# Statistics of the 2x2 sums moved in part beside the output projection, their loads into buffers of their own, and the order of the convolution's first loads

## The chip, the core and the metric

The kernel runs on one NeuronCore of a Trainium2 chip. The core has five engines that each work through an instruction stream of their own: TensorE (PE, matmul), VectorE (DVE), ScalarE (ACT), GpSimd (POOL) and SyncE (SP, which here only issues transfers). The metric is the device time of one execution in microseconds. The kernel before takes 3109.46 us, the median of three runs (3108.26 to 3110.49).

## What is computed

Two layers follow each other on one image `x` of 384 channels and 192 x 192 pixels in float32. Cut to what matters:

```python
# layer 0: attention over channels, on the group-normalised image, added to x
qkv = einsum(gn(x), w_qkv)                  # 1152 channels, then 2x2 max pooling to 96 x 96
q, k, v = split(depthwise_3x3(qkv))
out = sum_i topk_softmax(q @ k.T) @ v * a_i # 8 heads of 48 channels
out = repeat_2x2(gelu(out))                 # back to 192 x 192
x = x + einsum(out, w_proj) + b_proj
# layer 1: large-kernel depthwise convolution, on the group-normalised x, added to x
y = gn(x)
x = x + sum_i bn_i(depthwise(y, w_i))       # a 13 x 13 kernel and six smaller ones, folded into one
```

The second group norm needs mean and variance of the new `x`. The added term is constant over each 2x2 square, so the kernel gets the variance from three things: the variance of the old `x`, the statistics of the 2x2 sums of the normalised old `x`, and the statistics of these sums (scaled) plus the projection's output. No pass over the full-size new image is needed for it.

## The kernel before

Channels lie in three thirds of 128 partitions. The order of each stage is written out by hand, inside `manual_schedule` blocks; where such a block ends and another begins, the order on each engine is set when the kernel is built, and the waits with it. [...]Tiles come from pools of on-chip memory; the space of a closed pool is given to later pools, and the first user of the new tiles then waits for the last users of the old.

1. **Statistics** of `x` for the first norm.
2. **q, k, v** (`project`, L350): 1x1 projection, pooling, depthwise taps, Gram matrices, 48 blocks of rows twice over. Beside it GpSimd writes the 2x2 sums to DRAM (`sums`, L339).
3. **Attention stage** (L739 to L766): 24 blocks of four rows (`NBB` = 24, `NBK` = 384 pixels). For a block, PE multiplies four times (`av`, L747, two PSUM buffers for each), ACT applies Gelu (L756, L758) and writes three thirds back to `v`; the rest goes through a `gx` tile (three buffers), from which ACT copies one part (L761) and VectorE two (L763). VectorE also takes the statistics of the sums: `load_sums` (L716) reads all three thirds of a block into an `sm` tile (three buffers, loaded two blocks ahead), and three `bn_stats` (L766) follow the copies. After the blocks, L771 to L779 reduce them to `mvs`, `quarter` and `pre`. The weights `wp` of the next stage are loaded on SP between the second and the third `sm`.
4. **Projection** (L1058 to L1117): for each third `i` and block `b`, PE makes `pj` (three matmuls, L1067, three PSUM buffers), ACT writes `pj` plus bias to a `pjs` tile and to DRAM (`pd`), and VectorE makes `cell` = scaled sums plus `pj` (L1082) and its statistics (L1083). The sums come a second time, third by third, into five `smj` buffers of the pool `by` (`load_sum`, L1054), four loads ahead. `derive(i)` turns a third's statistics into the norm's scale and shift, in steps spread over the next third's blocks by `advance()`: its first step is an aggregate and an addition on VectorE (L834, L835), two blocks later comes a small matmul on PE (L106). `derive(2)` begins when the blocks are over and goes on beside the convolution. In the last third also the first two pieces of the convolution are made ready: rows are loaded (`load_rows`), the projection is added (`residual`), ACT normalizes them (`normalize1`, L963), VectorE transposes them (`arrange`, L978).
5. **Convolution** (L1136 to L1157): 48 pieces `k` of eight channels `c`. For a channel PE multiplies the folded taps `wt` with the transposed rows `xp` (L996) into one of four PSUM buffers, and ACT evicts it with a bias into `co` (L1004). For piece `k+1` or `k+2`, SP loads rows (`raw` from `x`, `up` from `pd`, 1.3 and 0.6 MB) and taps (1.6 MB), GpSimd adds (L955), ACT normalizes, VectorE transposes and adds the shift's term to the taps (`patch`, L945); GpSimd sends the output of the piece before. Taps 1 are the first load on SP after the projection, rows 2 follow.

## Time and profile before

| | |
|---|---|
| median of three runs | 3109.46 us |
| the profiled execution, its own time | 3107.91 us |
| its span (first to last instruction) | 3106.1 us |
| granted clock, mean | 0.997 |
| attention stage, first matmul | 1943.97 us after the span's start |
| projection, first matmul | 2010.70 us |
| convolution, first matmul | 2170.61 us |
| mean of a statistic L766 | 0.54 us |
| landing of a load: `sm`, `smj` (medians) | 5.0 us, 2.5 us |
| DMA busy share in the convolution, 2300 to 3075 us | 0.98 |

A row of a timeline is: start in us, length in us, engine, line, operation, output and input tiles, count of merged instructions, and in brackets the idle time of the engine just before it with what ended that. The profile counts each of these float32 matmuls as two records, so a block of the projection is six. In the answer by windows a row is: window, its length, busy time of the engine (records), the clock that was granted to TensorE (1.00 is full), the busy share of the DMA engines and GB/s.

### The profile page before, as it was taken

The page shows a single profiled execution, that of the slowest core. Times are in us where ns is not written, and L with a number is a line of the kernel's source. Part 1 is how long each engine was busy: PE and PEld are TensorE (multiplying, and loading weights), DVE is VectorE, ACT ScalarE, POOL GpSimd, SP SyncE. Part 2 cuts the span into 40 slices and gives each one's busy share as a digit, 9 for nine tenths or more (in the row PEclk, how much of TensorE's full clock was granted, in tenths as well). Part 3 has the DMA queues.
Part 4 walks back from the last instruction along what each step waited for, and adds up shares of the span by engine and source line. Part 5 has one row for each costly group of instructions (what it writes and reads, how often), then busy time and mean ns, then how long its engine had stood idle before and what let it go on. Part 6 is the DMA issues. An engine that isn't in the chain of part 4 may idle for free.

```text
span 3106.1 us, 31918 instructions
## 1 busy us (share of the span) xinstructions
PE 2917.1 (94%) x10794; PEld 1939.0 (62%) x10794; DVE 2523.7 (81%) x3453; ACT 1243.4 (40%) x2339; POOL 914.1 (29%) x1103
## 2 busy tenths in 40 slices
PE   0099999999999999999999999999999999999998
PEld 0056666666666666666555555555777777777776
DVE  8968787878787878888999999868778777777775
ACT  0034444444444444444444444623333333333332
POOL 3033232423232332312222222500333333333331
PEclk9999999999999999999999999999999999999999
DMA  9933433434242424333333332776999999999994
GB/s 387 379 112 99 132 116 112 136 95 153 80 151 78 154 88 142 106 117 112 105 100 100 129 102 69 215 218 198 258 264 248 244 244 247 247 249 242 243 219 116
DMA packets 279363, 528.67 MB, mean 170 GB/s; under 512 B 26850, under 2 KB 193824, under 8 KB 279200
## 3 DMA queue, kind: packets, MB, share of 16 engines
q1 hardware_dynamic: 207936, 331.72, 39.6%
q0 software_dynamic: 45040, 151.32, 16.1%
q10 hardware_dynamic: 26224, 43.59, 3.8%
q8 instruction: 86, 1.41, 0.2%
q14 instruction: 77, 0.63, 0.1%
HBM read 365.18 MB, written 161.37 MB: 170 GB/s over the span
## 4 chain that ended last, share of the span: by engine, by line
PE 85%; DVE 10%; DMA 3%; issue 1%; POOL 0%; ACT 0%; SPq 0%; DVEq 0%; ACTq 0%; POOLq 0%
PE qkv L350 49%; PE conv L996 28%; PE pj L1067 3%; DVE stats L236 3%; DVE v L397 3%; PE gram L438 2%; PE tr L426 2%; DVE mx L361 1%; DMA xs<-in_x 1%; DMA raw<-in_x 1%; PE av L747 1%; DMA xt<-in_x 1%; DVE stats_s L766 0%; DMA smj<-sums 0%; DVE cell L1082 0%
## 5 line engine op out<-in xcount | busy, mean ns | idle before, releaser
L350 PE MATMUL qkv<-xt,wqk 128*128 128x384 f32 x3456 | 1132.5, 487 | 1.3 <-ACT xt L327 1.3
L350 PEld LDWEIGHTS qkv<-xt,wqk 128*128 128x128 f32 x3456 | 650.3, 190 | 435.7 <-ACT xt L327 2.1
L996 PE MATMUL conv<-xp,wt 128*128 128x288 f32 (+1 forms) x3840 | 917.7, 402 | 2.5 <-ACT co L1004 2.5
L996 PEld LDWEIGHTS conv<-xp,wt 128*128 128x128 f32 x3840 | 729.0, 190 | 188.8 <-ACT co L1004 2.9
L397 DVE SCALAR_TENSOR_TENSOR acc<-pooled,wd,acc 128x384 f32<-128x384 f32 (+2 forms) x1152 | 732.2, 636 | 30.6
L361 DVE TENSOR_REDUCE mx<-qkv 128x192 f32<-128x768 f32 x432 | 412.6, 955 | 241.6 <-PE qkv L350 230.0
L978 DVE STREAM_TRANSPOSE xp<-xn 128x4608 f32<-128x4608 f32 (+1 forms) x107 | 441.9, 4130 | 185.5 <-PE conv L996 165.8
L368 ACT ACTIVATE pooled<-mx,bq 128x192 f32<-128x192 f32 x432 | 196.8, 456 | 962.0 <-DVE mx L361 961.7
L350 PE MATMUL qkv<-xt,wv 128*128 128x384 f32 x1728 | 563.8, 487 | 1.7 <-ACT xt L327 1.1
L350 PEld LDWEIGHTS qkv<-xt,wv 128*128 128x128 f32 x1728 | 325.6, 190 | 234.4 <-ACT xt L327 7.5
L1004 ACT ACTIVATE co<-conv,cb 128x288 f32<-128x288 f32 x384 | 191.3, 498 | 590.6 <-PE conv L996 590.6
L335 POOL TENSOR_TENSOR sum<-xt 128x192 f32<-128x192 f32 x144 | 96.9, 673 | 1110.4 <-ACT xt L327 1098.1
L397 DVE SCALAR_TENSOR_TENSOR v<-pooled,wd,v 128x384 f32<-128x384 f32 (+2 forms) x576 | 376.6, 654 | 15.2
L327 ACT ACTIVATE xt<-xt,gn 128x768 f32<-128x768 f32 x288 | 285.1, 1014 | 2.9 <-DVE gn L244 2.9
L1021 POOL DMA_DIRECT2D out<-o x191 | 105.8, 584 | 568.3 <-DVE o L1012 518.1
L955 POOL TENSOR_TENSOR raw<-raw,up 128x2496 f32<-128x2496 f32 x46 | 230.9, 5019 | 25.7 <-DMA raw<-in_x 18.3
L1012 DVE STREAM_TRANSPOSE o<-co 128x2304 f32<-128x2304 f32 (+1 forms) x50 | 209.7, 4197 | 19.8 <-ACT co L1004 19.8
L1067 PE MATMUL pj<-v,wp 128*128 128x384 f32 x432 | 146.8, 499 | 7.8 <-DVE cell L1082 5.9
L106 PE MATMUL g_ps<-mv,gm 128*32 128x1 f32 x18 | 1.8, 185 | 154.3 <-DVE mv L240 153.6
L1067 PEld LDWEIGHTS pj<-v,wp 128*128 128x128 f32 x432 | 82.8, 194 | 64.9 <-DVE cell L1082 6.7
L236 DVE BATCH_NORM_STATS2 stats<-xs 128x6 f32<-128x512 f32 x198 | 118.2, 674 | 2.7 <-DMA xs<-in_x 2.6
L336 POOL TENSOR_TENSOR sum<-sum,xt 128x192 f32<-128x192 f32 x144 | 113.3, 787 | 11.3
(170 smaller groups left out, 1718.5 us busy)
## 6 DMA issues: line engine op xcount, KB each, us to landing
xt<-in_x SPq DMA_DIRECT2D x96, 1152.0 KB, 7.4
wt<-zd SPq DMA_DIRECT2D x47, 1536.0 KB, 13.6
raw<-in_x SPq DMA_DIRECT2D x182, 312.0 KB, 13.5
out<-o POOLq DMA_DIRECT2D x188, 288.0 KB, 7.1
zd<-v POOLq DMA_DIRECT2D x96, 416.0 KB, 4.6
up<-pd SPq DMA_DIRECT2D x184, 156.0 KB, 12.4
xs<-in_x ACTq DMA_DIRECT2D x37, 768.0 KB, 13.3
xs<-in_x SPq DMA_DIRECT2D x29, 768.0 KB, 15.0
```

Source lines behind the costliest of these rows:

```text
L236: nc.vector.bn_stats(stats[:, j, NS0 + b * (FB // 512) + q, :], xt[:, q * 512 : (q + 1) * 512])
L327: nc.scalar.activation(xt[:, j], xt[:, j], AF.Identity, bias=gn0[:, j, 1:2], scale=gn0[:, j, 0:1])
L350: nc.tensor.matmul(ps[:, r, : 2 * W], lhsT=wq[:, j, mm * P : (mm + 1) * P], rhs=xt[:, j, r * 2 * W : (r + 1) * 2 * W], start=(j == 0), sto ...
L361: nc.vector.tensor_reduce(mx, ps[:, :, : 2 * W].rearrange("p r (y w x) -> p r w y x", y=2, x=2), AX.XY, ALU.max,)
L368: nc.scalar.activation(pool_t[m][:, k : k + SR, 1 : 1 + WS], mx, AF.Identity, bias=bq[:, m : m + 1])
L397: nc.vector.scalar_tensor_tensor(acc[:, :nt], pool_t[m][:, k0 + dy : k0 + dy + nt, dx : dx + WS], wd[:, m, t : t + 1], acc[:, :nt], ALU.mu ...
L955: eng.tensor_add(rv, rv, uv.unsqueeze(2).to_broadcast([P, (m1 - m0) * WS, 2]))
L978: nc.vector.transpose(bass.AP(at.tensor, at.offset, [list(at.ap[0]), [NBQ, n], [1, NBQ], [NQ * NBQ, CC], [ME * NBQ, NE]],), bass.AP(row.te ...
L996: nc.tensor.matmul(ps[:, t0:t1], lhsT=wt[:, c, o : o + P], rhs=d[:, c, g + 2 * t0 : g + 2 * t1 - 1 : 2, :], start=(g == 1), stop=(g == NGR ...
L1004: nc.scalar.activation(co[:, c], ps, AF.Identity, bias=cb[:, cc : cc + 1])
L1012: nc.vector.transpose(bass.AP(at.tensor, at.offset, [list(at.ap[0]), [2 * W, n], [BC, NBQ], [W, 2], [1, BC]]), bass.AP(of.tensor, of.offse ...
L1067: nc.tensor.matmul(ps, lhsT=wp[:, j, i * P : (i + 1) * P], rhs=v[:, j, b * RB : (b + 1) * RB, :].rearrange("p r w -> p (r w)"), start=(j = ...
```

## The change

There are four parts.

- Of the statistics of the sums, the attention stage takes only those of the second and third third; `sm` tiles shrink from three thirds to two. A block's `bn_stats` now stand two blocks after the load, ahead of the copies of that later block, and a load of block b stands behind the statistics of block b-2; the last two blocks' follow the loop.
- The first third's statistics are taken in the projection, on the `smj` tile that is there for `cell`. `stats_s` therefore lives on, in the pool `b2`, and each third's aggregate and three small operations move from behind the attention stage to the head of `derive`. The operations on constants go ahead of the stage.
- The `smj` buffers move from `by` to `b2`, and the first four loads are issued at the end of the attention stage.
- In the convolution, rows 2 are loaded ahead of taps 1; taps 1 come in two loads of four channels, and their `patch` moves from behind the first channel of piece 0 to its last two, half and half.

The diff, cut to its core:

```diff
+        stats_s = b2.tile([P, NJ, NBB, 6], F32, name="stats_s")
+        smj = {}
+
+        def load_sum(n):
+            i, b = divmod(n, NBB)
+            smj[n] = b2.tile([P, NBK], F32, tag="smj", name=f"smj_{n}", bufs=5)
+            nc.sync.dma_start(out=smj[n], in_=sums[i * P : (i + 1) * P, b * NBK : (b + 1) * NBK])
...
-            stats = b1.tile([P, NJ, NBB, 6], F32, name="stats_s")
             def load_sums(b):
-                sm = bx.tile([P, NJ, NBK], F32, tag="sm", name=f"sm_{b}")
+                sm = bx.tile([P, NJ - 1, NBK], F32, tag="sm", name=f"sm_{b}")
                 nc.sync.dma_start(
-                    out=sm, in_=sums[:, b * NBK : (b + 1) * NBK].rearrange("(j p) n -> p j n", p=P)
+                    out=sm, in_=sums[P:, b * NBK : (b + 1) * NBK].rearrange("(j p) n -> p j n", p=P)
                 )
                 return sm
+
+            def sum_stats(b):
+                sm = sms.pop(0)
+                for j in range(1, NJ):
+                    nc.vector.bn_stats(stats_s[:, j, b, :], sm[:, j - 1])
...
                 for b in range(NBB):
                     if b + 2 < NBB:
                         hxs.append(gather(b + 2))
-                        sms.append(load_sums(b + 2))
+                    if b >= 2:
+                        sum_stats(b - 2)
+                        sms.append(load_sums(b))
...
-                    sm = sms.pop(0)
-                    for j in range(NJ):
-                        nc.vector.bn_stats(stats[:, j, b, :], sm[:, j])
-            mvs = b1.tile([P, NJ, 2], F32, name="mvs")
-            for j in range(NJ):
-                nc.vector.bn_aggr(mvs[:, j, :], stats[:, j].rearrange("p n s -> p (n s)"))
...
+                for b in range(NBB - 2, NBB):
+                    sum_stats(b)
+                for n in range(4):
+                    load_sum(n)
...
         def derive(i, stats):
+            mvs = d1.tile([P, 2], F32, name="mvs", tag="mvs")
+            nc.vector.bn_aggr(mvs, stats_s[:, i].rearrange("p n s -> p (n s)"))
+            t = d1.tile([P, 1], F32, name="t", tag="t")
+            nc.vector.tensor_mul(t, mvs[:, 1:2], quarter[:, i : i + 1])
+            nc.vector.tensor_mul(t, t, quarter[:, i : i + 1])
+            nc.vector.tensor_sub(pre[:, i, 1:2], mv0[:, i, 1:2], t)
...
                     nc.vector.bn_stats(stats1[:, i, b, :], t)
+                    if i == 0:
+                        nc.vector.bn_stats(stats_s[:, i, b, :], sm)
...
         with tc.manual_schedule():
-            all_of(load_taps(1))
             patches(l2, 1)
             all_of(load_rows(2))
+            all_of(load_taps(1, n=CC // 2))
...
                             all_of(arrange(k + 1))
-                            patch(k + 1)
+                            if k > 0:
+                                patch(k + 1)
...
+                    if k == 0 and c >= CC - 2:
+                        patch(1, (c - CC + 2) * CC // 2, (c - CC + 3) * CC // 2)
```

More of the change, by code (lines that the diff above doesn't have):

```diff
@@ L733, in tile_attn_then_large_kernel_conv @@
             with tc.manual_schedule():
+                t = b1.tile([P, NJ], F32, name="t")
+                nc.vector.reciprocal(t, gn0[:, :, 0])
+                nc.vector.tensor_scalar(quarter, t, 0.25, None, ALU.mult)
+                nc.vector.tensor_mul(t, t, gn0[:, :, 1])
+                nc.vector.tensor_sub(pre[:, :, 0], bpj, t)
+                nc.vector.memset(mv1, 1.0)
                 hxs = [gather(b) for b in range(2)]
@@ L763, in tile_attn_then_large_kernel_conv @@
                             nc.vector.tensor_copy(of_block(c, b)[p], g[p])
-                    sm = sms.pop(0)
-                    for j in range(NJ):
-                        nc.vector.bn_stats(stats[:, j, b, :], sm[:, j])
-            mvs = b1.tile([P, NJ, 2], F32, name="mvs")
-            for j in range(NJ):
-                nc.vector.bn_aggr(mvs[:, j, :], stats[:, j].rearrange("p n s -> p (n s)"))
-            t = b1.tile([P, NJ], F32, name="t")
-            nc.vector.reciprocal(t, gn0[:, :, 0])
-            nc.vector.tensor_scalar(quarter, t, 0.25, None, ALU.mult)
-            nc.vector.tensor_mul(t, t, gn0[:, :, 1])
-            nc.vector.tensor_sub(pre[:, :, 0], bpj, t)
-            nc.vector.tensor_mul(t, mvs[:, :, 1], quarter)
-            nc.vector.tensor_mul(t, t, quarter)
-            nc.vector.tensor_sub(pre[:, :, 1], mv0[:, :, 1], t)
-            nc.vector.memset(mv1, 1.0)
+                for b in range(NBB - 2, NBB):
+                    sum_stats(b)
+                for n in range(4):
+                    load_sum(n)
         NK = C // CC
@@ L938, in load_taps, with patch @@
                 yield
-        def patch(k):
-            for c in range(CC):
+        def patch(k, lo=0, hi=CC):
+            for c in range(lo, hi):
                 cc = k * CC + c
@@ L1048, in tile_attn_then_large_kernel_conv @@
             with tc.manual_schedule():
-                smj = {}
-                def load_sum(n):
-                    i, b = divmod(n, NBB)
-                    smj[n] = by.tile([P, NBK], F32, tag="smj", name=f"smj_{n}", bufs=5)
-                    nc.sync.dma_start(out=smj[n], in_=sums[i * P : (i + 1) * P, b * NBK : (b + 1) * NBK])
-                for n in range(4):
-                    load_sum(n)
                 for n in range(NJ * NBB):
@@ L1081, in tile_attn_then_large_kernel_conv @@
                     t = by.tile([P, NBK], F32, tag="cell", name="cell", bufs=1)
-                    nc.vector.scalar_tensor_tensor(t, smj.pop(n), quarter[:, i : i + 1], ps, ALU.mult, ALU.add)
+                    sm = smj.pop(n)
+                    nc.vector.scalar_tensor_tensor(t, sm, quarter[:, i : i + 1], ps, ALU.mult, ALU.add)
                     nc.vector.bn_stats(stats1[:, i, b, :], t)
+                    if i == 0:
+                        nc.vector.bn_stats(stats_s[:, i, b, :], sm)
                     pd = pds[i]
```

## The prediction

> **What bounds the kernel now.** I read the page's busy shares and chain of waits first, then each engine's timeline from 1940 to 2220 us, the only stretch the diff touches, then the granted clock in 2 us windows.

> ```profile
> PE 2917.1 (94%) x10794; PEld 1939.0 (62%) x10794; DVE 2523.7 (81%) x3453; ACT 1243.4 (40%) x2339; POOL 914.1 (29%) x1103
> PE 85%; DVE 10%; DMA 3%; issue 1%; POOL 0%; ACT 0%; SPq 0%; DVEq 0%; ACTq 0%; POOLq 0%
> ```

> TensorE sets the end, so an edit is worth what it takes from PE's idle or slow time. PE's timeline in the stretch, by its lines with a wait, and one undisturbed row:

> ```profile
> 1961.83 0.86 PE L747 MATMUL av<-hx,bd 96*96 96x384 f32 x2 [0.18 <-ACT gx L758]
> 1968.88 0.86 PE L747 MATMUL av<-hx,bd 96*96 96x384 f32 x2 [1.43 <-ACT gx L758]
> 2010.70 7.77 PE L1067 MATMUL pj<-v,wp 128*128 128x384 f32 x18 [1.98 <-ACT gx L758]
> 2024.34 47.10 PE L1067 MATMUL pj<-v,wp 128*128 128x384 f32 x138 [5.87 <-DVE cell L1082]
> 2151.26 19.52 PE L1067 MATMUL pj<-v,wp 128*128 128x384 f32 x60
> 2197.07 12.19 PE L996 MATMUL conv<-xp,wt 128*128 128x288 f32 x50 [2.45 <-ACT co L1004]
> ```

> A projection block is six records: 1.94 us in the 60-record row, but 2.59 in the three blocks at 2010.70. VectorE explains the stalls:

> ```profile
> 1958.66 1.48 DVE L766 BATCH_NORM_STATS2 stats_s<-sm 128x6 f32<-128x384 f32 x3 [4.71 <-DMA sm<-sums]
> 1965.63 1.48 DVE L766 BATCH_NORM_STATS2 stats_s<-sm 128x6 f32<-128x384 f32 x3 [2.06 <-DMA sm<-sums]
> 2018.32 2.11 DVE L771 BATCH_NORM_AGGREGATE mvs<-stats_s 128x2 f32<-128x144 f32 x3
> 2023.67 0.62 DVE L1082 SCALAR_TENSOR_TENSOR cell<-smj,quarter,pj 128x384 f32<-128x384 f32 x1 [1.23 <-DMA smj<-sums]
> 2172.58 8.26 DVE L978 STREAM_TRANSPOSE xp<-xn 128x4608 f32<-128x4608 f32 x1
> ```

> It waits for sums at the start of the attention stage; its copies of gx stand behind that wait, ACT needs a gx buffer back, and PE needs ACT to empty its PSUM. From there VectorE runs late: its statistics end at 2018.4, then aggregates, then a load of smj issued only at 2021.15; meanwhile PE has filled its three PSUM buffers. Clock (window, PE busy, clock, DMA):

> ```profile
> 2011.00:2013.00 2.00, 2.00 (x6) 0.75 0.96 305
> 2013.00:2015.00 2.00, 2.00 (x5) 0.50 0.74 252
> 2025.00:2027.00 2.00, 2.00 (x4) 0.50 1.02 348
> ```

> And at the convolution's start:

> ```profile
> 2189.54 4.92 POOL L955 TENSOR_TENSOR raw<-raw,up 128x2496 f32<-128x2496 f32 x1 [18.33 <-DMA raw<-in_x]
> 2194.49 2.15 ACT L963 ACTIVATE xn<-raw,par 128x2112 f32<-128x2112 f32 x1 [8.87 <-DMA raw<-in_x]
> ```

> The third rows land late; ACT, in order, holds the evictions behind their normalization.

> [...]after 1.98 us of idle one dip of 3.4 us (2012.0 to 2015.4), after 5.87 us one of 6.8; but 2.45 us at 2194.6 gave none[...]. [...]the taps issued at 2170.80 went ahead, and the third rows landed by 2189.5.

> **The change part by part.**

> *Attention stage.* Two of three statistics stay: VectorE's work per block falls from 3x0.5+2x0.52=2.5 us to 2.0 (PE's pace is 2.58), two blocks behind the loads. In the built order the first sums wait no longer for VectorE's last tap (1953.95) but for ACT's pooled write (1944.4), so they land before use. The wp loads inherit that wait, and sm 2 stands behind wp on SP, so it stays near its 1961.2 issue, perhaps 2 us sooner; two blocks of lag cover it. PE's 24 blocks start 62.01 us apart, first to last; 23x2.583=59.4: saving 2.5.

> *The handover.* ACT's last gx then ends 0.5 us after PE, not 1.9: the 1.98 idle falls to 0.55, saving 1.4, and without its clock dip three blocks take 5.8 instead of 7.77: 1.95. The smj buffers are their own, so their four loads follow the last sm load on SP at once (320 ns each, nothing else queued behind but more of them), land in 2.5 us and are there before VectorE is free. In PE's new time (pj from 2006.8) VectorE ends copies at 2007.6, two pairs of statistics at 2009.6 (ACT's first pjs waits for these in the built order), constants at 2010.5, cell 0 at 2011.1; PE wants that buffer at 2012.6. The 5.87 goes, and its dip: 47.10-23x1.94=2.5. So far 2.5+1.4+1.95+5.87+2.5=14.2. If sm 23 came 1.5 us later than that, the gain would shrink from there one for one.

> *Statistics in the projection.* 24 of 0.5 us. VectorE was busy 29.4 of 47 us (2024 to 2071); 41.4 still fits: 1.3+0.5=1.8 against 1.94 per block. Cost nothing; without this cover it is at most 12.

> *derive.* Each call gains an aggregate (0.8) and three small operations (0.2 pitch): 1.4, in the path to the PE matmul L106. First call: plus 0.5 for the last statistics; mv was ready at 2070.47, PE came at 2071.37: 1.0 us of stall. Second: no slack (PE waited 0.67), but VectorE then waits 2.74 for smj and PE 1.14 at the next step, which take it up: 0.1. The constant operations moved ahead were already placed among the taps: nothing. mvs' three old aggregates are in the 5.87.

> *Convolution* (times counted from the old start of this stage, 2170.6). Rows and up 2 (1.9 MB) go first on SP, eight issues of 0.3 to 0.8 us, then taps 1 as two issues instead of one (0.4 more), then rows 3; POOL's queue is not touched. At the 200 to 300 GB/s of 2170 to 2190, and with about 2 us to land (smj: 2.5), rows 2 land near 2181 to 2183 instead of 2189.5, POOL adds 4.9, and ACT wants them after its sixth eviction, at 2185.6: the 2.45 goes. Taps 1 land by 2187 to 2189; their patch is eight operations of 0.2, and behind it on VectorE stands only the next transpose, which waits for ACT's normalization longer. PE wants the first patched tap at 2189.7 at the soonest, the fifth 9.5 us later: no wait. But the built order shows a new wait: the first eviction (co of k=0, c=0) now waits for the third derive's aggregate of stats_s, since stats_s lies in a pool whose space is given on to co's pool. On VectorE that aggregate stands behind the 8.26 us transpose (ends 2180.8) and a statistic (2181.2), so it ends at 2182.0. Behind it in ACT stand all evictions; PE with four PSUM buffers stops after c=3: 2170.61+4x2.385=2180.15, resumes at 2182.5: a stall of 2.35. After it PE wants taps 1 at 2192, and ACT rows 2 at 2187.8, so nothing is late next; rows landing as late as before would now do too. Gain 2.65 (the 2.45 and the slower restart) minus 2.35: 0.3.

> Sum: 14.2-1.0-0.1+0.3=13.4. Against the profiled execution (3107.91; span 3106.1, 1.8 around it) 3094.5. The median is 1.55 above that execution. New stalls of about 2 us, at the second derive and at the eviction, may each cost one dip, 1.7 us at half clock; with roughly even chances, less what later waits absorb, 1.4. So 3109.46-13.4+0.5 to 1.4, and I take 3096.5. Bounds of the unknown: no such dips and no eviction stall, 3109.46-15.8=3093.7 (3092.1 from the profiled execution); both dips and a second late transfer of about 2 us, 3099.5.

> **Rivals.**

> A (0.62), the sum above: 3096.5, own range 3093.5 to 3099.

> B (0.14), the eviction's wait doesn't bite, because VectorE gets the transpose or aggregate sooner: for it, VectorE is ahead of PE by more once the projection is unstalled; against it, the transpose needs the last normalization (ACT at 2170.7). 13.4+2.35: 3093.

> C (0.13), VectorE becomes the projection's bound: cell, two statistics and their semaphores take over 1.94 us. At 2.05 per block 24x0.11=2.6, plus a later derive, 1.5, and one dip: 3102. For it, 0.65 pitches in the timeline; against it, 0.73 us idle ahead of most cells now.

> D (0.07), the change doesn't free PE: sm 23 or smj 0 lands too late, as in the 2.74 wait; half of 5.87, both old dips and the even chances of new ones: 13.4-2.9-4.5-1.4=4.6, so 3104.9. It needs about 4 us of delay (cell 0 has 1.5 of slack), where the loads before took 4.2 to 6.0 us and now move two thirds.

> E (0.04), slower: the convolution's transfers bind. DMA's busy share is 0.98 from 2300 to 3075; if the reordered start leaves every one of 46 later rounds short, 0.4 us each is 18 us, net +5: 3114. It decides from 13.4/46=0.29 us a round. Against it: PE has no gap there, and the order of later loads is unchanged.

> **How the numbers follow.** From no change a measurement of this kernel can tell 0.2%, 6.2 us: 3103.2 and below is faster. A, B and most of C make faster 0.87; D and the rest same 0.09; E 0.04. The range 3092 to 3101.5 holds A, B and a little of C.

> **What would show it.** Right: attention blocks at 2.58 without ACT waits; pj within 0.7 us of av at full clock; no PE wait on cell; 1 us on L106 after the first third; one PE wait of 2.3 us on co, four blocks into the convolution, with ACT's co waiting for VectorE; no ACT wait on raw. Wrong: if cells crowd (C), if sm or smj shows as a releaser of VectorE near the handover (D), or if PE waits recur after 2230 (E).

## The result and the profile after

The changed kernel takes 3096.47 us (median of six runs, 3095.31 to 3097.91) against 3109.21 us of the kernel before beside it: a ratio of 0.9959 (95% interval 0.9946 to 0.9972). The profiled execution took 3095.74 us, with a span of 3094.0.

The page of the kernel after, busy time of the engines and shares of the chain that ended last:

```profile
PE 2913.6 (94%) x10794; PEld 1938.3 (63%) x10794; DVE 2529.4 (82%) x3459; ACT 1247.2 (40%) x2339; POOL 915.6 (30%) x1103
PE 87%; DVE 10%; DMA 1%; issue 1%; ACT 0%; POOL 0%; SPq 0%; ACTq 0%; DVEq 0%; POOLq 0%
```

PE's share of the chain has grown by two points and DMA's has fallen by as many. Two points are some 60 us, far more than the whole gain, so the chain has taken another path, and these shares don't price the change. VectorE does 5.7 us more work and the kernel is faster.

PE's timeline after, the rows that answer to those shown of before:

```profile
2006.83 50.58 PE L1074 MATMUL pj<-v,wp 128*128 128x384 f32 x156 [0.58 <-ACT gx L781]
2058.25 0.22 PE L106 MATMUL g_ps<-mv,gm 128*32 128x1 f32 x2 [0.84 <-DVE mv L851]
...
2109.53 0.22 PE L106 MATMUL g_ps<-mv,gm 128*32 128x1 f32 x2 [1.83 <-DVE mv L851]
2109.68 5.83 PE L1074 MATMUL pj<-v,wp 128*128 128x384 f32 x12
...
2170.61 26.50 PE L1012 MATMUL conv<-xp,wt 128*128 128x288 f32 x110 [2.48 <-ACT co L1020]
```

No row of the attention stage has a wait any more. The first 26 projection blocks are one row, at 1.945 us each: the wait on cell is gone and so are both clock dips. Three waits are new or longer: 0.84 us at the first derive, 1.83 at the second (0.67 before), 2.48 behind the convolution's fourth channel. After the second the two blocks of the 5.83 us row stand where 4.14 would do; the answer by windows shows why. PE idles 1.83 us in the first of them (1.58 busy of 3.41), and in the next the clock is at half:

```profile
2107.69:2111.10 3.41, 1.58 (x8) 1.00 1.07 267
2111.10:2114.52 3.42, 3.42 (x7) 0.50 1.06 271
```

VectorE, ACT and GpSimd in the timeline after:

```profile
1962.84 1.02 DVE L732 BATCH_NORM_STATS2 stats_s<-sm 128x6 f32<-128x384 f32 x2 [3.65 <-DMA sm<-sums]
2007.64 1.94 DVE L732 BATCH_NORM_STATS2 stats_s<-sm 128x6 f32<-128x384 f32 x4
2010.44 0.60 DVE L1090 SCALAR_TENSOR_TENSOR cell<-smj,quarter,pj 128x384 f32<-128x384 f32 x1
...
2170.05 1.67 ACT L1020 ACTIVATE co<-conv,cb 128x288 f32<-128x288 f32 x4 [10.24 <-DVE mvs L844]
2172.15 4.91 POOL L971 TENSOR_TENSOR raw<-raw,up 128x2496 f32<-128x2496 f32 x1 [13.13 <-DMA up<-pd]
```

VectorE still waits for the third `sm` load, but makes up for it; it ends the sums at 2009.6 and comes to cell 0 at 2010.4, where before it came at 2023.7. ACT's first four evictions leave together, once VectorE's aggregate of the third third is done. Rows 2 have landed 13.7 us after the convolution's start, 5.2 us sooner than before (18.9), though not as soon as the 10.4 to 12.4 us predicted; ACT waits 0.92 us for them, and PE doesn't.

By stages, from the first matmul of one to that of the next:

| us | before | after | saved |
|---|---|---|---|
| attention stage | 66.73 | 62.81 | 3.9 |
| projection, up to the first derive's matmul | 60.67 | 51.42 | 9.25 |
| projection, from there | 99.24 | 100.18 | -0.9 |
| convolution to the end of the span | 935.5 | 935.6 | -0.1 |

### The profile page after: what moved, and what is told of

The parts are those of the page before. It is cut to its first block, busy times and chain, and to the rows that moved or that the text cites. A ratio compares the mean times of both kernels' runs of the same rounds, so it can differ in the third digit from the quotient of the medians.

```text
span 3094.0 us, 31922 instructions
## 1 busy us (share of the span) xinstructions
PE 2913.6 (94%) x10794; PEld 1938.3 (63%) x10794; DVE 2529.4 (82%) x3459; ACT 1247.2 (40%) x2339; POOL 915.6 (30%) x1103
## 4 chain that ended last, share of the span: by engine, by line
PE 87%; DVE 10%; DMA 1%; issue 1%; ACT 0%; POOL 0%; SPq 0%; ACTq 0%; DVEq 0%; POOLq 0%
PE qkv L350 49%; PE conv L1012 29%; PE pj L1074 3%; DVE stats L236 3%; DVE v L397 3%; PE av L770 2%; PE gram L438 2%; PE tr L426 2%; DVE mx L361 1%; DMA xs<-in_x 1%; DMA xt<-in_x 1%; DVE xp L994 0%; DVE cell L1090 0%; DVE stats_t L1091 0%; DVE mv L240 0%
## 5 line engine op out<-in xcount | busy, mean ns | idle before, releaser
L106 PE MATMUL g_ps<-mv,gm 128*32 128x1 f32 x18 | 1.8, 186 | 156.3 <-DVE mv L240 153.6
```

## The experiments

The theory is the prediction's sum: VectorE's lateness at the handover cost PE its waits and clock dips, and in the convolution the new wait for the aggregate takes back what the sooner rows give. The rivals differ from run to run and stand with the expectations. Times are medians, with the ratio to the kernel before on the same chip; 0.001 of it is 3.1 us.

### The convolution's start

**The change without its reorder of loads.**

```diff
-            patches(l2, 1)
-            all_of(load_rows(2))
-            all_of(load_taps(1, n=CC // 2))
+            all_of(load_taps(1))
+            patches(l2, 1)
+            all_of(load_rows(2))
...
-                            if k > 0:
-                                patch(k + 1)
+                            patch(k + 1)
...
-                    if k == 0 and c >= CC - 2:
-                        patch(1, (c - CC + 2) * CC // 2, (c - CC + 3) * CC // 2)
```

> The changed kernel with the convolution's start as before (taps 1 first and whole, then rows 2, patch behind the first channel of piece 0). Theory (the first eviction's wait of 2.4 us delays everything by as much as the late rows did, so the reorder is worth nothing beside it): 3096.5 us, within 0.7, rows 2 landing 18 to 19 us after the stage's start without a PE stall of over 0.5 us there. Rival (the two waits add up): a second PE stall of 2.4 us on co, 3099.

Measured: 3096.93 us, 0.9961 (0.9949 to 0.9974): as the whole change. ACT's and PE's timeline:

```profile
2170.31 26.86 PE L1012 MATMUL conv<-xp,wt 128*128 128x288 f32 x110 [2.47 <-ACT co L1020]
2182.39 2.15 ACT L979 ACTIVATE xn<-raw,par 128x2112 f32<-128x2112 f32 x1 [6.51 <-POOL raw L971]
```

The rows land 19 us after the stage's start again, and ACT waits 6.51 us for them. PE, 2.47 us late already through the first eviction, no longer has a wait there: its 110 records take 0.36 us longer than after the change, and that is all.

**The kernel before with the reorder alone** (the same lines the other way round, with `patch(k, lo, hi)`).

> The kernel before with only the reordered start of the convolution. Its statistics of the sums lie in a pool that closes with the attention stage, so the first eviction has no wait for an aggregate. Theory: the 2.45 us PE wait on co goes, 3109.2-2.6=3106.6 (3106 to 3107.2). Rival (rows come no sooner, or PE waits for the patched taps instead): 3109.2.

Measured: 3105.6 us, 0.9988 (0.9982 to 0.9995), so 1.6 to 5.6 us faster than before and 0.4 below the expected range. PE's timeline at the projection's first wait on cell and at the start of the convolution:

```profile
2024.70 47.39 PE L1067 MATMUL pj<-v,wp 128*128 128x384 f32 x138 [7.47 <-DVE cell L1082]
...
2171.05 35.94 PE L996 MATMUL conv<-xp,wt 128*128 128x288 f32 x150
```

150 records without a wait, where before 100 and 50 had 2.45 us between them; the stage takes 3103.8 - 2171.05 = 932.75 us instead of 935.5. The reorder alone does what it says, and is worth 2.75 us in this profile.

The same profile says something of the handover, which this edit leaves as before. The 1.98 us wait is there, but no clock dip behind it (the three blocks take 6.07 us instead of 7.77), and the wait on cell is 7.47 us instead of 5.87. Cell 0 comes when VectorE comes to it, 12.9 to 13.0 us after PE's first projection matmul in both, so this dip only fills a part of a wait that is there anyway.

**The change with the sums' statistics in a pool of their own.**

```diff
-        stats_s = b2.tile([P, NJ, NBB, 6], F32, name="stats_s")
+        ls = ctx_l1.enter_context(tc.tile_pool(name="ls", bufs=1, side="right"))
+        stats_s = ls.tile([P, NJ, NBB, 6], F32, name="stats_s")
```

> The changed kernel with the statistics of the sums in a pool of their own at the other end of the memory, so that co's space holds no trace of them and the first eviction waits for the last cell only. Theory: the PE wait of 2.48 us four channels into the convolution goes and nothing takes its place, because rows 2 are normalized 21 us after the stage's start and PE can go on to 24: 3096.5-2.4=3094.1 (3093.5 to 3095). Rival (a later wait, for rows 2 or taps 1, takes its place): 3096.5.

Measured: 3092.95 us (3092.41 to 3093.46), 0.9948 (0.9935 to 0.996): 3.5 us less than the changed kernel's 3096.47, and 0.6 below the expected range.

```profile
2158.89 35.94 PE L1013 MATMUL conv<-xp,wt 128*128 128x288 f32 x150
2177.10 2.15 ACT L980 ACTIVATE xn<-raw,par 128x2112 f32<-128x2112 f32 x1 [3.19 <-DMA raw<-in_x]
```

PE's wait is gone, and nothing takes its place: ACT waits 3.19 us for rows 2, but is through with them before PE has run out of PSUM buffers. The convolution takes 3091.7 - 2158.89 = 932.8 us, as with the reorder alone. So the new wait came from where `stats_s` lies, not from the move of the aggregate itself, and it took back just what the reorder gave. The other 0.7 us fits the clock: this profile has the same 1.84 us wait at the second derive, with no dip behind it, and no dip can follow a wait that isn't there.

### The handover from attention to projection

**The kernel before with only the smj buffers in `b2`**, and their first four loads at the end of the attention stage.

```diff
+            smj[n] = b2.tile([P, NBK], F32, tag="smj", name=f"smj_{n}", bufs=5)
...
+                for n in range(4):
+                    load_sum(n)
```

> The kernel before with the smj buffers in the long-lived pool and the first four loads issued at the end of the attention stage; all else as before. Theory (VectorE is late because of its statistics and aggregates, the load only adds the last 1.23 us): the PE wait of 5.87 us on cell falls to 4.6, 3108 (3106.5 to 3108.7). Rival (the late load is the stall): wait and dip go, 3109.2-5.9-2.5=3100.8.

Measured: 3102.95 us, 0.9977 (0.9967 to 0.9986): 4 to 10 us faster, far more than the 1.2 of my theory and less than the rival. In its timeline (SPq rows are SP's issues):

```profile
1944.53 0.90 SPq L723 DMA_DIRECT2D sm<-sums  x2
...
2018.51 0.55 DVE L1082 SCALAR_TENSOR_TENSOR cell<-smj,quarter,pj 128x384 f32<-128x384 f32 x1
...
2019.11 46.41 PE L1067 MATMUL pj<-v,wp 128*128 128x384 f32 x138 [2.62 <-DVE cell L1082]
```

Before, SP issued the first two `sm` loads at 1954.14, after VectorE's last tap; here at 1944.53. Nothing in the diff touches these loads. The five smj buffers in `b2` push the `sm` tiles to other space, whose last user in the built order is ACT's pooled write, and PE has no wait in the attention stage although VectorE takes all three statistics. The stage is 64.65 us long instead of 66.73, so the tiles' place by itself is enough for most of the prediction's 2.5 us. The next run shows that it isn't needed for it. The wait on cell falls from 5.87 to 2.62; the statistics still end at 2016.5. The convolution starts 5.8 us sooner than before; in this profile 2.2 us of that go again there, to a longer wait for the rows (2.93 us) with a dip behind it.

**The change with the smj buffers in the projection's own pool, loads late** (the tile and the first four loads go back to `by`).

> The changed kernel with the smj buffers back in the projection's pool, so that their first loads wait until the attention stage's tiles are released. Theory (VectorE in time is what counts): the loads are issued at the last statistic, 2009.6 us, and land by 2012.3; PE waits 0.3 to 1.5 us on cell: 3097 (3096.3 to 3098.5). Rival (own buffers are the larger part): a stall of 4 us or more and a dip, 3101 or above.

Measured: 3097.52 us, 0.9957 (0.9945 to 0.997): as the change.

```profile
1956.32 0.88 SPq L718 DMA_DIRECT2D sm<-sums  x2
...
2007.80 50.73 PE L1075 MATMUL pj<-v,wp 128*128 128x384 f32 x156 [0.58 <-ACT gx L775]
...
2013.09 0.61 DVE L1091 SCALAR_TENSOR_TENSOR cell<-smj,quarter,pj 128x384 f32<-128x384 f32 x1 [2.58 <-DMA smj<-sums]
```

VectorE waits 2.58 us for the late load, and PE loses 0.15 (50.73 against 50.58). Early `smj` loads are worth next to nothing once VectorE is in time. The edit also moves the `sm` tiles: their first two loads are issued at 1956.32, even later than before (1954.14), and VectorE waits 3.49 and 2.62 us for sums. Still PE has no wait in the attention stage, which takes 62.81 us as in the change. So for this stage either is enough: loads that come sooner (the run above), or VectorE's smaller work two blocks behind its loads (this one).

**The change with all three thirds' statistics in the attention stage.**

```diff
-                sm = bx.tile([P, NJ - 1, NBK], F32, tag="sm", name=f"sm_{b}")
+                sm = bx.tile([P, NJ, NBK], F32, tag="sm", name=f"sm_{b}")
...
-                for j in range(1, NJ):
-                    nc.vector.bn_stats(stats_s[:, j, b, :], sm[:, j - 1])
+                for j in range(NJ):
+                    nc.vector.bn_stats(stats_s[:, j, b, :], sm[:, j])
...
-                    if i == 0:
-                        nc.vector.bn_stats(stats_s[:, i, b, :], sm)
```

> The changed kernel, but all three thirds of the sums' statistics stay in the attention stage (three to a block, two blocks after their load), none in the projection. Theory (the slack of 0.5 us per block is what is needed): VectorE has 2.5 of 2.58 us per block, can't make up for the 3.65 us it waits for the third load, ends some 4 us later, and PE waits 2 to 4 us on the first cells, with or without a clock dip: 3100 (3098 to 3103). Rival (the lag of two blocks alone does it): 3096 to 3097.

Measured: 3104.6 us, 0.9984 (0.9977 to 0.999): 8 us slower than the change, 4.6 more than the theory's middle and 1.6 above its range.

```profile
1965.23 1.48 DVE L732 BATCH_NORM_STATS2 stats_s<-sm 128x6 f32<-128x384 f32 x3 [4.88 <-DMA sm<-sums]
...
2020.46 46.35 PE L1074 MATMUL pj<-v,wp 128*128 128x384 f32 x138 [5.82 <-DVE cell L1090]
```

The wait for the third load is longer with three thirds (4.88 against 3.65 us). From it to the loop's last statistics, 2012.45, VectorE takes 47.2 us for 19 blocks, 2.49 each against PE's 2.58, so it makes up less than 2 us, and waits another 1.28 for the last sums: cell 0 comes 11.2 us after PE's first projection matmul, against 3.6 in the change. The wait on cell is back to 5.82 us with no dip ahead of it, where the run with the reorder alone, also without a dip there, had 7.47: most of the wait of before is back. In this profile the cell wait, the second derive and the eviction each have a dip behind them, so it stands 1.7 us above the median. So the lag of two blocks is not enough; the third that was moved out is what lets VectorE catch up.

**The first third's statistic taken twice.**

```diff
                     if i == 0:
                         nc.vector.bn_stats(stats_s[:, i, b, :], sm)
+                        nc.vector.bn_stats(stats_s[:, i, b, :], sm)
```

> The changed kernel with the first third's statistic in the projection taken twice (24 more of 0.5 us; the result is the same). Theory (VectorE needs 1.66 us of PE's 1.94 per block): 2.16 us per block is 0.22 over, 24 times is 5.2, part of it in the blocks and part at the first derive: 3101.7 (3100.5 to 3104). If VectorE already set the pace (the prediction's rival C): +12, 3108.5. If it had 0.5 us of slack or more: 3096.5 to 3097.

Measured: 3105.36 us, 0.9986 (0.9979 to 0.9992), 1.4 above the theory's range.

```profile
2007.85 54.06 PE L1074 MATMUL pj<-v,wp 128*128 128x384 f32 x156 [0.58 <-ACT gx L781]
2065.85 0.27 PE L106 MATMUL g_ps<-mv,gm 128*32 128x1 f32 x2 [3.94 <-DVE mv L851]
2066.05 6.86 PE L1074 MATMUL pj<-v,wp 128*128 128x384 f32 x12
```

Against the change PE loses 3.48 us in the blocks, 3.10 at the derive (3.94 against 0.84) and 2.72 in a clock dip behind that wait (6.86 against 4.14). The first two make 6.6 where I had 5.2: VectorE's pitch is 2.165 us to a block, so 0.22 over in each as expected, but the late first cell is never made up and the last block has one statistic more. The dip wasn't in the expectation. The prediction's rival C, that VectorE is the bound after one added statistic, is refuted: 0.28 us to a block were left, and it takes a second one to use them up.

### The derives, and a faster version

**Own pool, the first third's statistics two blocks ahead of their cell, the aggregates of the sums out of `derive`** (its first four operations become `sums_done`).

```diff
+                for n in range(2):
+                    nc.vector.bn_stats(stats_s[:, 0, n, :], smj[n])
                 for n in range(NJ * NBB):
...
+                    if n < NBB - 2:
+                        nc.vector.bn_stats(stats_s[:, 0, n + 2, :], smj[n + 2])
+                    if n in (NBB - 2, NBB + 11, NBB + 13):
+                        sums_done((NBB - 2, NBB + 11, NBB + 13).index(n))
...
-                    if i == 0:
-                        nc.vector.bn_stats(stats_s[:, i, b, :], sm)
```

> The changed kernel with three edits: the sums' statistics in a pool of their own (no eviction wait), the first third's statistics taken two blocks ahead of their cell, and each third's aggregate of the sums taken out of derive into blocks 22, 35 and 37 of the projection. Theory: -2.4 at the eviction, -0.84 at the first derive, -1.2 at the second, and -0 to -1.7 for the clock dip behind it: 3091 (3089.8 to 3092.7). Rival (the waits at the derives only move to the next step): 3094.

Measured: 3093.41 us, 0.9945 (0.9932 to 0.9959): no better than the own pool alone, and above the theory's range.

```profile
2008.60 0.56 DVE L1069 BATCH_NORM_STATS2 stats_s<-smj 128x6 f32<-128x384 f32 x1 [2.08 <-DMA smj<-sums]
...
2014.46 44.77 PE L1079 MATMUL pj<-v,wp 128*128 128x384 f32 x138 [1.09 <-DVE cell L1099]
```

The wait at the first derive is gone and the second is down to 0.68, but the first statistic was put ahead of the attention stage's last copies and waited 2.08 us for its load, and PE then waits 1.09 us on cell. A wait on `g_sb` grew to 1.17 us (0.17 with the own pool alone).

**The changed kernel again**, beside the two that follow:

> The changed kernel once more, as the measure for the two versions beside it: 3096.5 us, within 1.

Measured: 3096.97 us, 0.9957 (0.9944 to 0.9969).

```profile
2108.93:2112.35 3.42, 2.16 (x8) 1.00 1.07 253
2112.35:2115.76 3.41, 3.41 (x14) 1.00 1.05 265
...
2170.15 28.19 PE L1012 MATMUL conv<-xp,wt 128*128 128x288 f32 x110 [2.48 <-ACT co L1020]
```

The waits are the same as in the first profile of it (1.84 and 2.48 us), but here the second derive has no dip behind it and the eviction has one (28.19 against 26.50). The clock's record explains both. In each profile every change of the clock lies a whole number of 3.413 us from every other (in that of before the dips are 3.413 and 6.827 us long, and 10.240 us from start to start), so time falls into windows of that length. Where they begin differs between executions, by 1.25 us between these two, counted from the span's start. Here a boundary cuts the 1.84 us wait into 0.58 and 1.26, as the first two lines show for the larger part, while the 2.48 us wait lies in one window. In the first profile the 1.83 us wait lay in one window, and the 2.48 was cut into 1.00 and 1.48.

**The same, going ahead only from block 8 on.**

```diff
-                for n in range(2):
-                    nc.vector.bn_stats(stats_s[:, 0, n, :], smj[n])
...
-                    if n < NBB - 2:
-                        nc.vector.bn_stats(stats_s[:, 0, n + 2, :], smj[n + 2])
+                    if 8 <= n < NBB:
+                        for m in range(n + (n > 8) + (n > 16), min(n + 1 + (n > 15), NBB - 1) + 1):
+                            nc.vector.bn_stats(stats_s[:, 0, m, :], smj[m])
...
+                    if n < 8:
+                        nc.vector.bn_stats(stats_s[:, 0, n, :], sm)
```

> As the version with the early aggregates (statistics in a pool of their own, aggregates of the sums taken out of derive, now in blocks 23, 35 and 37), but the first third's statistics go ahead of their cell only from block 8 on, one block, and two from block 16 on, so that none stands at the handover. Theory (the 1.09 us PE wait on cell came from statistics at the handover that waited 2.08 us for their load): against 3093.0 of the version with the own pool alone, -0.84 at the first derive, -1.16 at the second, +1.0 for the wait on g_pc that VectorE's wait for a late smj brings back: 3092 (3091.2 to 3092.6). Rival (the aggregates only move the work): 3093 or more.

Measured: 3090.76 us (3090.62 to 3091.51), 0.9938 (0.9925 to 0.9952): on this chip 6.2 us less than the change, and 0.4 below the expected range. From the attention stage's first matmul to the convolution's the profile is 1.1 us shorter than that of the own pool alone (212.00 against 213.10), which is what the theory gave; the rest of the difference lies ahead of this stretch.

```profile
2006.86 50.58 PE L1077 MATMUL pj<-v,wp 128*128 128x384 f32 x156 [0.57 <-ACT gx L782]
2057.37 0.22 PE L106 MATMUL g_ps<-mv,gm 128*32 128x1 f32 x2
...
2123.72 0.60 PE L134 MATMUL g_pc<-g_sb,gmt 32*128 32x2 f32 x4 [0.91 <-DVE g_sb L129]
```

The first 26 blocks are undisturbed, the first derive has no wait, the second 0.67 us; 0.91 on `g_sb` and 1.31 on `par` are left. The cause of the 1.09 us was the statistics at the handover: without them it is gone.

**One block more between three pairs of `derive`'s steps** (a further `yield` ahead of the matmuls on `mv`, `g_sb` and `sv`).

> As the version that goes ahead later, with one block more between the steps of derive at three places: before the matmul on mv, before that on g_sb and before that on sv. Theory (PE's waits at the second derive, 0.68, 1.17 and 1.31 us, are latency of VectorE's chain, not a lack of VectorE's time): -3.0, 3089 (3088.3 to 3090.3). Rival (VectorE has no time left in the last third, and the waits come back on cell or at the convolution's start): 3091.5 or more.

Measured: 3091.24 us, 0.9939 (0.9926 to 0.9951): nothing gained, and above the theory's range. The three waits are gone, and a long one is new:

```profile
2121.26 0.26 PE L123 MATMUL g_pv<-g_s,gm 128*32 128x1 f32 x4 [2.68 <-DVE g_s L118]
```

VectorE comes late to `g_s` because it waits 2.62 and 1.07 us for `smj` loads.

**Seven smj buffers, loads six blocks ahead.**

> As the version with longer steps in derive, with seven smj buffers and loads six blocks ahead instead of five and four. Theory (the last wait in the projection, 2.68 us of PE on g_s, comes from smj loads that crawl while the second pieces' rows are loaded at full DMA share; two blocks, 3.9 us, more lead than VectorE's largest wait of 2.62 us covers it): 3091.2-2.7=3088.5 (3087.7 to 3089.7). Rival (under that traffic a lead of any size runs dry, the loads come at a lower rate than VectorE takes them): 3090.5 or more.

Measured: 3090.05 us, 0.9937 (0.9923 to 0.995), not to be told from the two before it; it lies between the theory's range and the rival's. ACT's timeline (ACTq is its issue of a store):

```profile
2116.80 0.37 ACTq L1106 DMA_DIRECT2D pd<-pjs  x1
2117.22 0.58 ACT L1088 ACTIVATE pjs<-pj,bpj 128x384 f32<-128x384 f32 x1 [4.95 <-DMA pd<-pjs]
```

VectorE no longer waits for `smj`, and PE's wait on `g_s` is still 2.15 us: VectorE waits 3.03 us for ACT, and ACT 4.95 for an earlier store of `pjs` (the eviction before ended at 2112.27, its own store is issued only at 2116.80, and the next eviction stands behind that issue). The rows of the second piece are being loaded then, at a DMA share of 1.05. Loads and stores are late alike, so my theory for this run named one of two victims (ACT's waits of 3.05 and 3.87 us for stores stood in the trace of the run before), and neither more lead nor longer steps removes the traffic. Why both are late at once no run here shows. Loading these rows at another time wasn't tried.

## Why the prediction was right

**Attention stage and handover drain** (2.5 + 1.4 predicted, 3.9 measured). The size held, the credit only in part: I gave it to the smaller work of VectorE and to the sooner loads together. For the waits within the stage either alone is enough: with the buffers alone, all three statistics in place, it loses them and 2.1 us, and with the `smj` buffers in the projection's pool, where the first `sm` loads come late, it loses them too. The lighter VectorE is what brings the 1.98 us wait at the stage's end down to 0.58, and it is needed to be in time for cell 0, as the run with three thirds in the attention stage shows.

**Cell, the dips, and the first derive** (1.95 + 5.87 + 2.5 - 1.0 = 9.3 predicted, 9.25 measured). The first two are one term: without the dip the wait is longer by as much (7.47 us with the reorder alone), so removing the dip alone would have saved nothing. As both go, the sum holds. VectorE's dates came as worked out: copies to 2007.6, sums to 2009.6, cell 0 at 2010.4 (2011.1 predicted; one constant fell behind it). The slack for a late load was real: one that came 2.6 us late cost 0.15.

**Statistics in the projection at no cost.** Right: 1.66 us needed of 1.94, a second statistic costs 6.6 us and a dip.

**Second derive** (-0.1). The wait on `mv` grew by 1.16 us and those after it fell by 1.8 (1.14, 0.50 and 0.15): 0.6 gained in one profile, 0.1 in the other.

**Convolution** (+0.3: 2.65 less 2.35). Measured 2.75 less 2.48 and 0.3 of slower restart, -0.1. The runs that undo one side each find both terms: the reorder alone saves 2.75, the own pool for the statistics gives 2.8.

**New dips** (1.4). Each of the two profiles of the change has one, of 1.7 us, one behind the second derive and one behind the eviction. Where the wait falls in a window decides: 1.83 us within one window had a dip behind it, 1.84 us cut into 0.58 and 1.26 had none. The prediction's even chances were its author's estimate, somewhat low for the longer wait (the last section works them out).

Sum: 13.4 less 1.4 is 12.0 us; the spans differ by 12.1. That the median came within 0.03 us of the forecast is luck: the sum itself leads to 3096.6 to 3097.5, the forecast of 3096.5 lies just below that, and the six runs are spread over 2.6 us. Rival A came in. B fell with the 2.48 us wait, C with 0.27 us of idle time ahead of the cells, D because the one wait for sums, at 1962.84, is far from the handover, E because PE has no wait from 2170.61 to the end. What failed was not in the prediction but in the later theories: nine of the twelve runs fell outside their expected range, most by 0.4 to 1.6 us. One reason is that twice I charged one cause with a wait that had two, the buffers at the handover and the loads at the second derive; another, for the statistic taken twice, is a clock dip that I had left out.

## What to carry to other kernels

Moving a tile to a longer-lived pool moves its neighbours: look in the built order at what the first user of every tile of that region now waits for, both at the start (here 9.6 us sooner for a load the diff doesn't touch) and where the pool's space is given on (here 2.5 us later for the first eviction, free to mend). An engine that must recover from one late load needs slack per block, so count it before taking work off or on: 0.3 us to a block was enough in the projection, 0.1 too little in the attention stage. Where two parts of a change are each enough to remove a wait, undoing one of them shows nothing; run each alone as well. When waits are taken away one by one and the next in line stays about as long, look for the traffic that all of them share.
